# An expert tile's bias addition moved behind the next tile's first products, and three weight buffers instead of two

## The chip, the cores and the metric

The kernel runs on one core of a Trainium2 chip. The metric is the device time of one execution in microseconds, the median of three runs. A core has TensorE (PE in the profile; its weight loads are PEld), VectorE (DVE), ScalarE (ACT), GpSimd (POOL), SyncE (SP) and 16 DMA engines. Each engine executes its own queue of instructions in order, and engines wait for each other by semaphores.

## What is computed

The input x has four images of 256 channels and 64 by 64 pixels. Each image is normalised over its channels and goes through three modulated deformable 3x3 convolutions with a relu, and is added to x. Then every pixel is a token of 256 numbers: it is normalised, a gate picks its two best of eight experts, and each of the two contributes a two-layer network weighted by its gate value.

```python
def _deform_layer(x, w_off, b_off, w, b, dilation=1):
    om = lax.conv_general_dilated(x, w_off, ...) + b_off[None, :, None, None]
    off = om[:, :2 * K].reshape(B, K, 2, H, W)
    mask = jax.nn.sigmoid(om[:, 2 * K:])
    ...
    sampled = _bilinear(x, ys, xs) * mask[:, None]
    out = jnp.einsum('bikhw,oik->bohw', sampled, wk) + b[None, :, None, None]

x = x + _L0_conv_ref(_ln_c(x), ...)          # three of these layers, relu after each
t = _ln_t(_to_tokens(x))
probs = softmax(t @ gate_w + gate_b); top2_vals, top2_idx = top_k(probs, 2)
for each expert e:
    h = gelu(t @ W1[e] + b1[e]); y = h @ W2[e] + b2[e]
    out = out + cw[:, e] * y
x = _from_tokens(_to_tokens(x) + out)
```

All numbers are fp32.

## The kernel before

**Stages.** The convolution work is cut into 12 stages of one layer of one image, in the order of `stages` (line 1037): (0,0), (1,0), (0,1), (2,0), (1,1), (0,2), (2,1), (1,2), (0,3), (2,2), (1,3), (2,3), written as (layer, image). A stage has 8 blocks of 512 pixels; a block runs over 9 taps, a tap over 4 samples of 128 pixels. So a stage has 288 samples, and the run 3456.

**One sample** (`samples`, line 494): POOL issues an indirect DMA that gathers four corners for 128 pixels into a gather buffer g (L503; the pool `gat` has GB = 10 of them), VectorE sums the corners in two steps (L509, L514) into a buffer s (8 of them), ScalarE scales s in place (L517). Two samples are transposed on TensorE (`turn`, L532) and copied by ScalarE into sT (L535), and after four samples come the accumulating products with the layer's weights (`finish`, L555). `turn` is written LAG = 2 pairs behind the samples.

**Expert tiles.** When the third layer of an image is done its tokens are routed. The list of (token, expert) pairs, sorted by expert and padded, is cut into tiles of 256 rows: NF = 39 tiles for a whole image (groups 0, 1, 2) and 23 for each half of the last image (groups 3 and 4), 163 tiles in all. `begin` (line 968) puts each tile's generator `expert` into the lane `tiles` in three pieces, one every pace/3 taps; the pace is 5, 5, 2, 1.5 and 0 taps per tile for the five groups. Where no taps are left to run beside (`drain`, line 1021, called by `settle` and at the end) pieces are taken one after the other, and `draining` is set. The pieces of a tile are:

1. the bias addition of the tile before (`products`, L892, VectorE, from PSUM tile py to y) with the store of y on SP's queue (L895); then the transposes of the tile's 256 gathered tokens (L840) and ScalarE's copy fzT (L844);
2. when draining, the fetch for the next tile; then the first products ph (L856) and the Gelu hT (L866);
3. when not draining, the fetch for the next tile; then the second products py (L874).

`fetch` issues three indirect DMAs on POOL's queue: the weights of the tile's expert, both layers and biases, 9232 bytes a partition (L800), and two times 128 token rows zt (L812). The weight buffer w is one of two, by the parity of the step. A list `same` marks the tiles whose expert is that of the tile before them in the same stream; their row index lies beyond the bound, and nothing is moved. So that two streams can keep their weights, the list is worked on as two halves, alternating: `order` is tile 0, half, 1, half + 1 and so on, and `same` is set to 0 at the start of each half.

The py tile in PSUM is single (`ps1` has one buffer), so a tile's second products wait for the addition of the tile before. A weight buffer is free when its last reader, the addition with the bias of the second layer, is done.

**Order.** The code is traced by a framework that turns it into one queue per engine: it orders instructions by priority and readiness in its own plan, so an engine's order can differ from that of the code. `after(x)` keeps the instructions in its block behind x on their engine: the additions stand behind the newest sample's L514 (`self.last`), the fetches behind the newest gather (`self.gathered`).

The pool `wt` holds the weight tiles; before the first tile its buffers serve as windows of the convolution's input (`window`, line 281) in the first stage. In the first blocks the pool `gat` also lends buffers (`room`, line 188).

Of the kernel before, what the change touches and what calls it, by code (L numbers as in the profile page):

```python
# [34 lines left out]
FT_LOG = 8  # L35
FT = 1 << FT_LOG
FU = FT // P
GB = 10
LAG = 2
LEAST = 2.0**-30  # L40
WINN = CC * (RPB + 2) * W
W1N = CC * HID + HC
W2N = HC * C + C
# [39 lines left out]
class Group:  # L83


    def __init__(self, b, n0, n1):
        self.b, self.n0, self.n1 = b, n0, n1
        self.nm = f"{b}_{n0}"
        self.M = (n1 - n0) * TPB

        self.NF = 2 * self.M * P // FT + E - 1


        self.half = (self.NF + 1) // 2
        self.zt, self.acc, self.gy, self.sums, self.py = {}, [], [], [], None
        self.order = [s // 2 + s % 2 * self.half for s in range(self.NF)]


class Lane:
# [18 lines left out]
class Weave:  # L118
# [3 lines left out]
    def __init__(self, ctx, tc, ins, out):  # L122
        nc = self.nc = tc.nc
        self.tc = tc
        self.ins = ins
        self.x = ins["x"].rearrange("b (c p) h w -> b p c (h w)", p=P)
        self.out_v = out.rearrange("b (c p) h w -> b p c (h w)", p=P)
        self.B = self.x.shape[0]

        def pool(name, bufs, **kw):  # L130
            return ctx.enter_context(tc.tile_pool(name=name, bufs=bufs, **kw))

        self.cst = pool("cst", 1)
        self.dram = pool("dram", 1, space=bass.MemoryType.DRAM)
        self.wkp = pool("wkp", 1)
        self.plan = pool("plan", 19)
        self.win = pool("win", 3)
        self.wt = pool("wt", 2)
        self.small = pool("small", 1)
        self.big = pool("big", 2)  # L140
        self.ffn = pool("ffn", 2)
        self.rt = pool("rt", 1)
        self.rt2 = pool("rt2", 2)
        self.gyp = pool("gyp", 4)
        self.smT = pool("smT", 2)
        self.smp = pool("smp", 8)
        self.gat = pool("gat", GB)
        self.ps = pool("ps", 3, space=bass.MemoryType.PSUM)
        self.ps1 = pool("ps1", 1, space=bass.MemoryType.PSUM)

        self.routes, self.tiles, self.sums = Lane(), Lane(), Lane()
        self.side, self.plans_side = [], []
        self.last = self.gathered = self.turned = None
        self.starting, self.draining, self.later = True, False, []
        self.pend, self.pairs = None, []
# [534 lines left out]
    def route(self, grp):  # L690

        nc, M, NF = self.nc, grp.M, grp.NF
# [4 lines left out]
        def small(tag, shape, dt=F32):  # L697
            return self.rt.tile(list(shape), dt, tag=tag, name=f"{tag}_{grp.nm}")
# [52 lines left out]
        nc.vector.tensor_scalar(rows, ex, float(P), self.part, ALU.mult, ALU.add)  # L751
        same = small("same", (P, NF))
        nc.vector.tensor_tensor(same[:, 1:], ex[:, 1:], ex[:, : NF - 1], ALU.is_equal)
        nc.vector.memset(same[:, 0 : grp.half + 1 : grp.half], 0.0)
        nc.vector.scalar_tensor_tensor(rows, same, float(E * P), rows, ALU.mult, ALU.add)
        nc.vector.tensor_copy(grp.wrow, rows)

# [32 lines left out]
    def fetch(self, grp, step):  # L790

        if self.w is None:
            self.w = [
                self.wt.tile([P, 2, WINN], F32, tag="wt", name=f"w_{i}").rearrange(
                    "p a b -> p (a b)"
                )
                for i in range(2)
            ]
        f = grp.order[step]
        self.nc.gpsimd.indirect_dma_start(  # L800
            out=self.w[step % 2][:, : W1N + W2N],
            out_offset=None,
            in_=self.ins["W"],
            in_offset=bass.IndirectOffsetOnAxis(ap=grp.wrow[:, f : f + 1], axis=0),
            bounds_check=E * P - 1,
            oob_is_err=False,
        )
        grp.zt[step] = []
        for u in range(FU):
            zt = self.ffn.tile([P, C], F32, tag=f"zt{u}", name=f"zt_{grp.nm}_{f}_{u}")  # L810
            j = FU * f + u
            self.nc.gpsimd.indirect_dma_start(  # L812
                out=zt,
                out_offset=None,
                in_=grp.zd,
                in_offset=bass.IndirectOffsetOnAxis(ap=grp.tok[:, j : j + 1], axis=0),
            )
            grp.zt[step].append(zt)
# [6 lines left out]
    def expert(self, grp, step):  # L825

        nc = self.nc
        if step == 0:
            self.fetch(grp, 0)
            yield  # L830
        self.products(grp)
        f = grp.order[step]
        nm = f"{grp.nm}_{f}"
        w = self.w[step % 2]
        w1, w2 = w[:, :W1N], w[:, W1N : W1N + W2N]
        zt = grp.zt.pop(step)
        tp = self.ps.tile([P, CC, FT], F32, tag="tp", name=f"ftp_{nm}")
        for u in range(FU):
            for c in range(CC):
                nc.tensor.transpose(  # L840
                    tp[:, c, u * P : (u + 1) * P], zt[u][:, c * P : (c + 1) * P], self.ident
                )
        zT = self.ffn.tile([P, CC, FT], F32, tag="zT", bufs=1, name=f"fzT_{nm}")
        nc.scalar.copy(zT, tp)  # L844
        yield

        beside = not self.draining
        if not beside:
            self.fetch_next(grp, step)
        hT = []  # L850
        for h0 in range(0, HC, 2):
            ph = self.ps1.tile([P, 2, FT], F32, tag="ph", name=f"ph_{nm}_{h0}")
            for h in range(2):
                for c in range(CC):
                    o = c * HID + (h0 + h) * P
                    nc.tensor.matmul(  # L856
                        ph[:, h, :],
                        lhsT=w1[:, o : o + P],
                        rhs=zT[:, c, :],
                        start=(c == 0),  # L860
                        stop=(c == CC - 1),
                    )
            ht = self.ffn.tile([P, 2, FT], F32, tag="hT", bufs=3, name=f"hT_{nm}_{h0}")
            for h in range(2):
                k = CC * HID + h0 + h
                nc.scalar.activation(ht[:, h, :], ph[:, h, :], AF.Gelu, bias=w1[:, k : k + 1])  # L866
            hT.append(ht)
        yield
        if beside:
            self.fetch_next(grp, step)  # L870
        py = self.ps1.tile([P, FU, C], F32, tag="py", name=f"py_{nm}")
        for u in range(FU):
            for h in range(HC):
                nc.tensor.matmul(  # L874
                    py[:, u, :],
                    lhsT=hT[h // 2][:, h % 2, u * P : (u + 1) * P],
                    rhs=w2[:, h * C : (h + 1) * C],
                    start=(h == 0),
                    stop=(h == HC - 1),
                )  # L880
        grp.py = (f, py, w2)
# [254 lines left out]
```

## Time and profile before

| what | us |
|---|---|
| runs before | 7508.25 median of 3 (7496.17 to 7528.83) |
| profiled execution, whole | 7520.62 |
| its span, first to last instruction | 7518.9 |
| first addition y (L892) starts | 2377.0 |
| last gather (L503) issued | 7065.8 |
| last addition y starts | 7465.8 |

The mean granted clock of TensorE is 0.944. An engine's busy time is the time in which it executes something; "idle before" is its idle time just ahead of an instruction, put down to what ended it. "remote" and "another core or an unknown queue" mean that the profile does not name who ended a wait. Start times of the samples show the stages:

| stage | from | to | tiles' additions |
|---|---|---|---|
| (1,0), (0,1), (2,0) | 657 | 2110 | 0 |
| (1,1) | 2110 | 2652 | 7 |
| (0,2), (2,1), (1,2) | 2652 | 4472 | 39 |
| (0,3), (2,2) | 4472 | 5645 | 29 |
| (1,3) | 5645 | 6396 | 26 |
| (2,3) and the drain behind it | 6396 | 7519 | 62 |

### The profile page before, as it was taken

To read this page: it belongs to the slowest core of one execution; us is meant where nothing else is said; L and a number is where in the kernel's file an instruction comes from. 1 tells how busy PE (TensorE), PEld (TensorE's weight loads), DVE (VectorE), ACT (ScalarE), POOL (GpSimd) and SP (SyncE) were. 2 spreads that over 40 slices of the span, in tenths; PEclk is the share of its full clock that TensorE was granted. 3 is DMA by queue.
4 is the path that set the end of the run, shared out by engine and by line. 5 is a ranking of instruction groups with operands and counts; after the bars stand their busy time and mean duration, and the time that the engine had idled before them with its cause. 6 is when DMAs were issued, how large, how long until landed. Compare 5 with 4: busy or idle time off the path is not lost.

```text
span 7518.9 us, 88985 instructions
## 1 busy us (share of the span) xinstructions
PE 6443.2 (86%) x26500; PEld 3618.8 (48%) x26500; DVE 4952.9 (66%) x11467; ACT 3266.0 (43%) x7141; POOL 4476.5 (60%) x4245
## 2 busy tenths in 40 slices
PE   6898888888898888889988888888888788977887
PEld 3443333334454444445554445444544555644565
DVE  6776777768887666567777556666768554667421
ACT  3444544445544444445443434444444333444322
POOL 4654666656666565556557656555656565666543
PEclk8999999999999999999999999999999899989998
DMA  8997999989998888888888888888888777888644
GB/s 266 337 325 274 352 342 335 346 331 356 362 349 311 300 305 297 278 315 322 314 293 316 293 280 314 295 302 294 308 306 299 251 271 240 288 302 287 211 139 123
DMA packets 800320, 2223.73 MB, mean 296 GB/s; under 512 B 104729, under 2 KB 302873, under 8 KB 794081
## 3 DMA queue, kind: packets, MB, share of 16 engines
q0 software_dynamic: 551200, 1947.35, 73.3%
q1 hardware_dynamic: 248640, 270.69, 10.9%
q8 instruction: 215, 3.52, 0.2%
q14 instruction: 265, 2.16, 0.1%
HBM read 2160.68 MB, written 196.40 MB: 313 GB/s over the span
## 4 chain that ended last, share of the span: by engine, by line
PE 69%; ACT 10%; issue 7%; another core or an unknown queue 6%; DVE 4%; DMA 2%; POOL 1%; SPq 0%; ACTq 0%; DVEq 0%; POOLq 0%
PE acc L555 34%; PE tp L532 10%; PE ph L856 7%; PE py L874 6%; PE po L357 6%; ACT sT L535 4%; ACT s L517 3%; DVE g L509 2%; DVE s L514 1%; PE pm L371 1%; ACT hT L866 1%; PE ftp L840 1%; ACT win L577 1%; PE tpv L325 1%
## 5 line engine op out<-in xcount | busy, mean ns | idle before, releaser
L503 POOL DMA_INDIRECT g<-tab,idx x3456 | 3685.4, 1066 | 2371.6 <-DVE s L514 1061.8
L555 PE MATMUL acc<-sT,wk 128*128 128x512 f32 x6912 | 3492.1, 620 | 253.4 <-ACT sT L535 147.5
L509 DVE SCALAR_TENSOR_TENSOR g<-g,cf 128x512 f32<-128x512 f32 x3456 | 2559.2, 742 | 269.1 <-DMA g<-tab,idx 245.5
L514 DVE SCALAR_TENSOR_TENSOR s<-g,cf 128x256 f32<-128x256 f32 x3456 | 1662.7, 483 | 1331.3 <-PE tp L532 729.9
L535 ACT COPY sT<-tp 128x512 f32<-128x512 f32 x1728 | 1002.0, 585 | 2312.0 <-PE tp L532 1553.0
L517 ACT ACTIVATE s<-s,cf 128x256 f32<-128x256 f32 x3456 | 1629.5, 508 | 256.7 <-DVE s L514 160.7
L555 PEld LDWEIGHTS acc<-sT,wk 128*128 128x128 f32 x6912 | 1198.9, 198 | 1106.7 <-issue 816.7
L532 PEld LDWEIGHTS tp<-ident,s 128*128 128x128 f32 x6912 | 893.2, 146 | 1666.2 <-issue 898.9
L532 PE MATMUL tp<-ident,s 128*128 128x128 f32 x6912 | 1287.3, 286 | 439.2 <-ACT s L517 253.8
L856 PE MATMUL ph<-fzT,w 128*128 128x256 f32 x2608 | 720.8, 411 | 78.0 <-ACT fzT L844 28.1
L874 PE MATMUL py<-w,hT 128*128 128x256 f32 x2608 | 671.1, 396 | 103.5 <-ACT hT L866 58.0
L856 PEld LDWEIGHTS ph<-fzT,w 128*128 128x128 f32 x2608 | 506.3, 205 | 212.9 <-issue 69.6
L874 PEld LDWEIGHTS py<-w,hT 128*128 128x128 f32 x2608 | 484.5, 196 | 242.0 <-issue 91.9
L866 ACT ACTIVATE hT<-ph,w 128x256 f32<-128x256 f32 x652 | 281.9, 471 | 616.3 <-PE ph L856 378.2
L812 POOL DMA_INDIRECT zt<-z,tok x326 | 333.8, 1024 | 161.5 <-issue 88.0
L800 POOL DMA_INDIRECT w<-in_W,wrow x163 | 178.0, 1092 | 381.2 <-issue 138.8
L357 PE MATMUL po<-win,wo 128*32 128x504 f32 (+1 forms) x2304 | 366.0, 615 | 6.5 <-ACT win L301 4.2
L892 DVE TENSOR_TENSOR y<-py,w 128x512 f32<-128x512 f32 x163 | 111.9, 686 | 341.5 <-PE py L874 285.1
L915 POOL DMA_INDIRECT gy<-ys,slots x256 | 255.6, 998 | 104.5 <-issue 70.0
L930 DVE SCALAR_TENSOR_TENSOR ta<-gy,cw,ta 128x256 f32<-128x256 f32 x256 | 120.6, 480 | 125.6 <-DMA gy<-ys,slots 78.4
L357 PE MATMUL po<-win_pre,wo 128*32 128x504 f32 (+1 forms) x1152 | 184.2, 617 | 2.0 <-ACT om L366 2.0
L366 ACT ACTIVATE om<-po,bo 128x512 f32<-128x512 f32 x96 | 65.9, 687 | 265.3 <-PE po L357 156.3
(154 smaller groups left out, 2961.0 us busy)
## 6 DMA issues: line engine op xcount, KB each, us to landing
tab<-hv SPq DMA_DIRECT2D x512, 128.0 KB
g<-tab,idx POOLq DMA_INDIRECT x3456
ys<-y SPq DMA_DIRECT2D x163, 256.0 KB
tab<-h_pre SPq DMA_DIRECT2D x128, 256.0 KB
wk<-in_conv_w SPq DMA_DIRECT2D x99, 256.0 KB
xc_pre<-in_x SPq DMA_DIRECT2D x32, 512.0 KB
xr_tok<-in_x SPq DMA_DIRECT2D x32, 512.0 KB
t<-t_tok SPq DMA_DIRECT2D x32, 512.0 KB
```

Of the source, the lines that this page charges most:

```text
L357: nc.tensor.matmul(po[g * Q : (g + 1) * Q, :].rearrange("q (r w) -> q r w", w=W)[:, :, x0:x1], lhsT=self.wo[l][:, 3 * ky + kx, c, :], rhs= ...
L503: self.gathered = nc.gpsimd.indirect_dma_start(out=g.rearrange("p x s f -> p (x s f)"), out_offset=None, in_=self.table(*self.stages[i]), ...
L509: nc.vector.scalar_tensor_tensor(g[:, :, 0, :], g[:, :, 1, :], cf[:, j, 0:1], g[:, :, 0, :], ALU.mult, ALU.add,)
L514: self.last = nc.vector.scalar_tensor_tensor(s, g[:, 1, 0, :], cf[:, j, 1:2], g[:, 0, 0, :], ALU.mult, ALU.add)
L517: nc.scalar.activation(s, s, AF.Copy, scale=cf[:, j, 2:3])
L532: self.turned = nc.tensor.transpose(tp[:, c, u * P : (u + 1) * P], ss[u][:, c * P : (c + 1) * P], self.ident)
L535: nc.scalar.copy(self.sT[:, :, t0 * P : (t0 + 2) * P], tp)
L555: nc.tensor.matmul(acc[:, o, :], lhsT=self.wk[k][:, c, o * P : (o + 1) * P], rhs=sT[:, c, :], start=(k == 0 and c == 0), stop=(k == K - 1 ...
L812: self.nc.gpsimd.indirect_dma_start(out=zt, out_offset=None, in_=grp.zd, in_offset=bass.IndirectOffsetOnAxis(ap=grp.tok[:, j : j + 1], axi ...
L856: nc.tensor.matmul(ph[:, h, :], lhsT=w1[:, o : o + P], rhs=zT[:, c, :], start=(c == 0), stop=(c == CC - 1),)
L866: nc.scalar.activation(ht[:, h, :], ph[:, h, :], AF.Gelu, bias=w1[:, k : k + 1])
L874: nc.tensor.matmul(py[:, u, :], lhsT=hT[h // 2][:, h % 2, u * P : (u + 1) * P], rhs=w2[:, h * C : (h + 1) * C], start=(h == 0), stop=(h == ...
```

## The change

The list of tiles is worked on as three thirds, alternating, with three weight buffers; the gather pool has 9 buffers instead of 10. The addition of the tile before moves from the head of a tile's first piece to the head of its third, just ahead of the second products, with its store. The fetch for the next tile always stands at the head of the second piece, whether draining or not.

```diff
-GB = 10
+GB = 9
...
-        self.half = (self.NF + 1) // 2
+        self.third = -(-self.NF // 3)
...
-        self.order = [s // 2 + s % 2 * self.half for s in range(self.NF)]
+        self.order = [s // 3 + s % 3 * self.third for s in range(self.NF)]
...
-        self.wt = pool("wt", 2)
+        self.wt = pool("wt", 3)
...
-        nc.vector.memset(same[:, 0 : grp.half + 1 : grp.half], 0.0)
+        nc.vector.memset(same[:, 0 : 2 * grp.third + 1 : grp.third], 0.0)
...
-                for i in range(2)
+                for i in range(3)
...
-            out=self.w[step % 2][:, : W1N + W2N],
+            out=self.w[step % 3][:, : W1N + W2N],
...
         if step == 0:
             self.fetch(grp, 0)
             yield
-        self.products(grp)
         f = grp.order[step]
...
-        w = self.w[step % 2]
+        w = self.w[step % 3]
...
         nc.scalar.copy(zT, tp)
         yield
 
-        beside = not self.draining
-        if not beside:
-            self.fetch_next(grp, step)
+        self.fetch_next(grp, step)
         hT = []
...
             hT.append(ht)
         yield
-        if beside:
-            self.fetch_next(grp, step)
+        self.products(grp)
         py = self.ps1.tile([P, FU, C], F32, tag="py", name=f"py_{nm}")
```

## The prediction

> **What bounds the kernel now.** I read the page's busy shares first, then the same shares by stage, then the waits of VectorE and TensorE, then the lines of the change.
>
> ```profile
> PE 6443.2 (86%) x26500; PEld 3618.8 (48%) x26500; DVE 4952.9 (66%) x11467; ACT 3266.0 (43%) x7141; POOL 4476.5 (60%) x4245
> ```
>
> TensorE is the fullest engine. The stages tell whether it also sets the pace where the expert tiles run (columns: window, length, busy time of PE, PEld, DVE, ACT, POOL with counts, granted clock, DMA share, GB/s).
>
> ```profile
> 657.00:1129.00 472.00, 392.57 (x1457) 177.27 (x1452) 346.08 (x677) 219.46 (x484) 310.71 (x292) 0.96 0.93 343
> ...
> 2652.00:3240.00 588.00, 512.38 (x2087) 284.99 (x2086) 357.89 (x706) 257.59 (x574) 343.87 (x331) 0.96 0.86 295
> ...
> 5850.00:6400.00 550.00, 480.97 (x2058) 305.49 (x2057) 276.78 (x551) 215.04 (x485) 324.67 (x323) 0.94 0.77 260
> 6400.00:6660.00 260.00, 241.62 (x1031) 168.40 (x1030) 162.71 (x336) 116.13 (x255) 155.68 (x156) 0.97 0.85 293
> 6660.00:6920.00 260.00, 197.07 (x719) 105.59 (x718) 194.10 (x498) 106.65 (x222) 168.63 (x154) 0.90 0.87 300
> 6920.00:7067.00 147.00, 120.84 (x509) 84.70 (x507) 80.14 (x187) 57.75 (x123) 87.57 (x84) 0.94 0.74 251
> ```
>
> The first row is a stage without expert tiles (TensorE 83%), the second one with 15 (87%), the next two hold the dense tiles at a pace of 2 and 1.5 taps (87%, 93%), the fifth a routing phase without tiles, the last the end before the drain (82%). The last gather is issued at 7067; from there the tiles run alone.
>
> What a tile costs is read from the drain, in the timeline of VectorE:
>
> ```profile
> 7212.83 0.69 DVE L892 TENSOR_TENSOR y<-py,w 128x512 f32<-128x512 f32 x1 [7.56 <-PE py L874]
> 7221.03 0.69 DVE L892 TENSOR_TENSOR y<-py,w 128x512 f32<-128x512 f32 x1 [7.51 <-PE py L874]
> 7229.23 0.69 DVE L892 TENSOR_TENSOR y<-py,w 128x512 f32<-128x512 f32 x1 [7.51 <-PE py L874]
> ```
>
> A tile every 8.2 us. Fifteen tiles make 123 us, and 588 less 472 is 116: a stage with tiles is a stage without them plus TensorE's tiles. TensorE sets the pace; an idle VectorE is paid for only where TensorE runs dry too.
>
> **What the change aims at.** The bias addition waits for TensorE, with VectorE's gathered sums queued behind it. Total, times and longest wait, over the run:
>
> ```profile
> DVE y L892 <- PE py L874: 285.1, 49, 13.6
> DVE g L509 <- DMA g<-tab,idx: 245.5, 90, 10.9
> ```
>
> The same line cut at 7067 gives 100.8 us (20 times) before and 184.4 us after. After it, no sample is queued behind the addition: the 184.4 us cost nothing. Of the 100.8, all lie behind 5645, where the pace is 2 or 1.5 taps.
>
> **Part by part.**
>
> (a) *Addition later.* In the built order of group 2, 34 of 39 additions stand 9 samples behind the last sample transposed before their products; the new order has 8 at 9, 25 at 10 to 13. Eight buffers hold the scaled samples, so VectorE leads TensorE's transposes by at most 8: at 10 the products have always ended, at 9 they may not. Three quarters of the wait in this group goes. For groups 0 and 1 the distance goes from 13 to 21, where nothing waited. The bound is 0 to −100.8 us. TensorE is at 87 to 93% where most of these waits lie, no less than the 83 to 87% of stages without them; only the 147 us before the drain are low, at 82%. At 86% they would be 147 × 0.04 = 6 us shorter. I take −6. The wait removed from VectorE then becomes its wait for free sample buffers (L514 on the transposes, already 729.9 us), which is TensorE again.
>
> The Trainium skill ("Perfetto Trace Analysis", Identifying the Most-Contended Engine) says that matmul busy time is a bad measure of how full TensorE is, and names the weight loads' share instead. That share is 48% here, which would leave TensorE half free, make VectorE's 66% the fullest, and put the whole 100.8 us on the path: about 7407 us. The stage arithmetic above speaks against it here.
>
> (b) *Third weight buffer, fetch one piece earlier.* POOL's order decides: the weight fetch (L800) stands in POOL's queue with the gathers behind it, and waits until its buffer's last reader, an addition, is done. Before, at pace 2 and 1.5, the fetch stands 4 gathers behind that addition; in the new order, with three buffers, it still stands 4 behind it, since the addition has moved back by the piece count that the third buffer gives. At pace 5 it goes from 12 to 16, of 9 or 10 gather buffers: no stall either way. So POOL's lead over VectorE stays short in the dense stages (median 7.9 us from the end of a gather's issue to its use in stage (1,3), against 12.5 to 16 us in the others), and the 227.7 us of waits for gathers behind 5645 stay. Effect 0. Per tile POOL issues the same three fetches (L800 once, L812 twice; 163 and 326 in all), each about 1.05 us, one piece earlier; behind them in the queue only the order changes. In the drain, where no gather separates them, the weights can be fetched a tile of 8.2 us earlier. What they cost there:
>
> ```profile
> PE otp L948 <- issue: 20.5, 10, 3.3
> PE otp L948 <- DVE ta L930: 16.6, 6, 8.4
> PE py L874 <- ACT hT L866: 14.9, 21, 7.9
> PE ph L856 <- DMA w<-in_W,wrow: 14.2, 4, 7.6
> ```
>
> That is TensorE's waits behind 7067: 14.2 us in four waits, the bound of the gain. I take −12. Against it stands a forced third weight load at the start of each group (five more loads in the run). In the dense stages it lies beside TensorE; in the drain's one or two groups I take +4, half a wait of 7.6 us (bounds 0 and 2 × 7.6 = 15). Together −8, between −14 and +15.
>
> (c) *Second products later.* In groups 0 and 1 the old order begins a tile's second products as soon as the Gelu allows, and TensorE waits 43 us for the Gelu before 7067 (23.6 behind 5645, 19.5 before). The new order begins them 8 to 12 samples later (the second tile's behind sample 1315 instead of 1307), right behind the addition, long after the Gelu. Bound 0 to −43. What they filled elsewhere is lost, so I take a quarter: −10.
>
> (d) *New wait of TensorE for VectorE.* The products now stand right behind an addition that VectorE executes 1 or 2 samples later than the last transposed one. Behind the products in TensorE's queue lie the transposes and the accumulation (L532, L555). Where VectorE leads by several samples, the addition is over. Where TensorE has caught up, VectorE needs 0.74 + 0.48 + 0.69 = 1.91 us (L509, L514, L892) while ACT's 0.51 and four transposes of 0.15 take 1.1 us: 0.8 us a tile. The 729.9 us that VectorE waits for transposes show it ahead nearly everywhere. Bounds 0 and 125 tiles before the drain × 0.8 = +100; taken +2, the row nearest (TensorE's wait for y in the drain, 2.3 us).
>
> (e) *Nine gather buffers.* Where the lead is 12.5 to 16 us, one of ten buffers is one sample period, 472/288 = 1.64 to 606/288 = 2.1 us. Transfers there waited for (short leads) landed in 3 to 4 us. The cover is that lead; 0 taken. Without it each of the 90 waits for a gather could grow by 2.1 us: +189 us of VectorE, nothing below 0.
>
> (f) *Windows.* The third buffer is also free for the pre-windows of stage (0,0), where VectorE waited 10.0 us once at L292; between 0 and −10, taken −1, TensorE being the bound.
>
> SP's store of y (0.4 us an issue, 163) moves with the addition. SP waits there 1152.2 us in 80 waits for y, with table stores and weight taps behind; a shorter wait of y shortens this one. Taken 0.
>
> Sum: −6 − 8 − 10 + 2 + 0 − 1 = −23 us. The profiled execution took 7520.6 us (span 7518.9): 7498. The runs' median is 7508.25, 12 us lower; from it 7485 us, which I predict.
>
> **Rivals.** *Nothing reaches TensorE* (7508): (a) to (c) are all idle time of engines off the path. For it: 93% at 6400 in spite of the waits. Against: the drain's 14.2 us are on TensorE itself.
>
> *The starved stages pay* (7428): TensorE runs dry wherever VectorE waits there, and gets it all back; 7508 − 100.8, and + 20.7 for the 8 of 39 places still at 9 samples. For it: gathers wait longest exactly where y waits. Against: TensorE's share there.
>
> *TensorE waits for the addition* (7583): (d) at three quarters of its upper bound, +75. Its place is the first of the second products of each tile; it decides where VectorE leads by fewer than 2 samples. For it: TensorE waits for scaled samples already (140.7 us between 2304 and 5645), so it does catch up. Against: those waits are 88, on some 800 transposed pairs.
>
> **Chances and range.** Forecast 0.45, nothing reaches TensorE 0.18, starved stages pay 0.17, TensorE waits for the addition 0.20. A measurement of this kernel tells about 0.5%, 38 us, from no change (its runs spread from 7496 to 7529). With ±25 us around each case, faster by more (below 7471): 0.17 of the second rival but for a hundredth, plus 0.3 of the forecast, 0.30; slower (above 7546): 0.20; within: 0.50. The likeliest case's own range is 7455 to 7515. The range 7418 to 7576 leaves out some 0.18, parts of both outer rivals.
>
> **What would show it.** Right: y's wait before 7067 falls from 100.8 to about 30 us; fetch L800 still ends long waits in stages (1,3) and (2,3); waits for w in the drain shrink from 14.2 us; stages without tiles keep 472, 481 and 500 us. Wrong: a new row "PE py waits for DVE y" of tens of us; waits for gathers in stages before 5645; or TensorE's share above 90% in the last third and a time below 7455.

## The result, and the profile after

The changed kernel takes 7557.56 us (median of 9 runs, 7536.64 to 7588.9), the kernel before, run beside it, 7500.98 us (9 runs, 7487.89 to 7528.83). The ratio is 1.0073, with a 95% interval of 1.0052 to 1.0095: slower by 0.7%, 55 us. The forecast was 7485 us, a gain of 0.3%.

The page's first line after the change, by engine, reads almost as before:

```profile
PE 6452.2 (85%) x26500; PEld 3620.0 (48%) x26500; DVE 4954.1 (66%) x11467; ACT 3270.2 (43%) x7141; POOL 4484.4 (59%) x4245
```

The loss is found by cutting the span into four: up to stage (1,3), stage (1,3), stage (2,3) up to the last gather, and the drain. Before (columns as in the prediction's table of stages):

```profile
97.00:5645.00 5548.00, 4815.27 (x19533) 2543.25 (x19534) 3916.08 (x8930) 2554.22 (x5588) 3399.39 (x3181) 0.95 0.89 316
5645.00:6396.00 751.00, 642.32 (x2699) 400.30 (x2701) 435.37 (x969) 297.37 (x654) 445.85 (x427) 0.93 0.78 265
6396.00:7066.00 670.00, 563.54 (x2280) 360.78 (x2268) 438.44 (x1022) 282.27 (x604) 413.98 (x397) 0.94 0.83 286
7066.00:7519.00 453.00, 358.63 (x1574) 282.92 (x1574) 105.25 (x285) 104.49 (x232) 190.61 (x195) 0.88 0.44 135
```

After:

```profile
97.00:5652.00 5555.00, 4812.56 (x19520) 2537.71 (x19520) 3916.98 (x8931) 2556.48 (x5590) 3403.85 (x3181) 0.95 0.89 315
5652.00:6431.00 779.00, 649.58 (x2694) 404.91 (x2694) 434.51 (x967) 296.30 (x653) 444.33 (x428) 0.91 0.75 257
6431.00:7116.00 685.00, 574.96 (x2318) 369.04 (x2318) 443.47 (x1035) 288.03 (x611) 421.82 (x399) 0.93 0.82 283
7116.00:7552.00 436.00, 349.17 (x1546) 275.52 (x1544) 101.57 (x271) 101.72 (x225) 187.39 (x192) 0.89 0.45 139
```

The four lengths change by +7, +28, +15 and −17 us: the drain pays, and the two stages in which tiles come every 2 or 1.5 taps take it back more than twice.

What becomes of VectorE's waits in stage (1,3) says why nothing was won there. Before (engine, what waited and for whom, total us, times, longest):

```profile
DVE g L509 <- DMA g<-tab,idx: 143.1, 38, 10.9
DVE y L892 <- PE py L874: 44.9, 9, 7.7
...
DVE s L514 <- PE tp L532: 18.2, 8, 9.2
...
DVE s L514 <- remote: 15.2, 6, 6.8
```

After:

```profile
DVE s L514 <- remote: 99.5, 30, 9.7
DVE s L514 <- PE tp L532: 74.3, 33, 9.7
DVE g L509 <- DMA g<-tab,idx: 51.6, 29, 5.2
DVE y L888 <- PE py L870: 29.9, 4, 10.9
```

The waits for gathers fall by 91.5 us and those for the addition by 15. The waits ahead of L514, which needs a free sample buffer, grow by 140.4 us, of which the profile names TensorE for 56.1 and no one ("remote") for 84.3: VectorE now has more of its samples and stands, as far as it is named, behind TensorE. The stage itself takes 28 us longer, and TensorE's longest waits there name ScalarE:

```profile
PE tp L532 <- ACT sT L535: 23.2, 8, 8.7
PE tp L532 <- ACT s L517: 20.9, 13, 8.4
PE ph L853 <- ACT fzT L843: 19.8, 5, 7.5
```

Before, they were 3.5, 7.1 and 4.5 us. Over the stages with tiles (2304 to the last gather) TensorE's waits for scaled samples go from 174.2 to 216.0 us, and those of the window products for the copies sT from 56.8 to 69.1.

One of e3's six executions below took 9271.97 us at a granted clock of 0.657, and no ratio uses it.

### The profile page after: what moved, and what is told of

The parts are those of the page before. It is cut to its first block, busy times and chain, and to the rows that moved or that the text cites. A ratio compares the mean times of both kernels' runs of the same rounds, so it can differ in the third digit from the quotient of the medians.

```text
span 7552.5 us, 89157 instructions
## 1 busy us (share of the span) xinstructions
PE 6452.2 (85%) x26500; PEld 3620.0 (48%) x26500; DVE 4954.1 (66%) x11467; ACT 3270.2 (43%) x7141; POOL 4484.4 (59%) x4245
## 4 chain that ended last, share of the span: by engine, by line
PE 67%; ACT 9%; issue 8%; another core or an unknown queue 7%; DVE 5%; DMA 2%; POOL 1%; SPq 0%; ACTq 0%; DVEq 0%; POOLq 0%
PE acc L555 33%; PE tp L532 10%; PE ph L853 7%; PE py L870 6%; PE po L357 6%; ACT sT L535 4%; ACT s L517 3%; DVE g L509 2%; DVE s L514 1%; PE pm L371 1%; DMA g<-tab,idx 1%; ACT hT L863 1%; ACT win L577 1%; PE tpv L325 1%
## 5 line engine op out<-in xcount | busy, mean ns | idle before, releaser
L514 DVE SCALAR_TENSOR_TENSOR s<-g,cf 128x256 f32<-128x256 f32 x3456 | 1662.7, 483 | 1516.2 <-PE tp L532 791.5
L853 PE MATMUL ph<-fzT,w 128*128 128x256 f32 x2608 | 683.5, 402 | 84.1 <-ACT hT L863 28.0
L870 PE MATMUL py<-w,hT 128*128 128x256 f32 x2608 | 631.7, 391 | 37.9 <-ACT hT L863 23.6
```

The source lines that it names most:

```text
L514: self.last = nc.vector.scalar_tensor_tensor(s, g[:, 1, 0, :], cf[:, j, 1:2], g[:, 0, 0, :], ALU.mult, ALU.add)
L853: nc.tensor.matmul(ph[:, h, :], lhsT=w1[:, o : o + P], rhs=zT[:, c, :], start=(c == 0), stop=(c == CC - 1),)
L870: nc.tensor.matmul(py[:, u, :], lhsT=hT[h // 2][:, h % 2, u * P : (u + 1) * P], rhs=w2[:, h * C : (h + 1) * C], start=(h == 0), stop=(h == ...
```

## The experiments

The runs come in five sets. Each set ran on one chip, with the kernel before beside it, and each on a chip of its own. Times of different chips are not compared here, only ratios to the kernel before on the same chip. The times are medians; the ratios are estimated from all runs of a set and lie up to 0.0014 from the quotients of the medians.

| run | kernel | us | before, us | ratio | 95% interval |
|---|---|---|---|---|---|
| e1 | 9 gather buffers alone | 6810.84 | 6807.77 | 1.0009 | 1.0001 to 1.0018 |
| e2 | third weight buffer alone | 6741.08 | 6807.77 | 0.9904 | 0.9888 to 0.9919 |
| e3 | third buffer, fetch early | 6767.65 | 6807.77 | 0.9944 | 0.9930 to 0.9959 |
| e4 | third buffer, addition late | 6779.70 | 6807.77 | 0.9964 | 0.9951 to 0.9977 |
| e5 | the changed kernel | 7559.43 | 7504.93 | 1.0068 | 1.0055 to 1.0082 |
| e6 | as e2 | 7482.22 | 7504.93 | 0.9974 | 0.9961 to 0.9987 |
| e7 | changed, addition at the end of piece 2 | 7543.75 | 7504.93 | 1.0040 | 1.0025 to 1.0055 |
| e8 | changed, second products in halves | 7528.52 | 7504.93 | 1.0032 | 1.0018 to 1.0046 |
| e9 | as e3 | 7676.29 | 7632.82 | 1.0057 | 1.0035 to 1.0079 |
| e10 | as e4 | 7609.09 | 7632.82 | 0.9966 | 0.9945 to 0.9986 |
| e11 | e2, second products in one stretch | 7645.88 | 7632.82 | 1.0014 | 0.9994 to 1.0035 |
| e12 | e8, fetch where it stood | 7614.04 | 7632.82 | 0.9979 | 0.9955 to 1.0003 |
| e13 | the changed kernel | 7646.00 | 7628.17 | 1.0009 | 0.9985 to 1.0032 |
| e14 | as e2 | 7583.46 | 7628.17 | 0.9937 | 0.9915 to 0.9960 |
| e15 | as e3 | 7667.15 | 7628.17 | 1.0053 | 1.0032 to 1.0075 |
| e16 | as e4 | 7597.00 | 7628.17 | 0.9964 | 0.9942 to 0.9986 |
| e17 | changed, window products ordered | 6674.27 | 6810.04 | 0.9804 | 0.9791 to 0.9818 |
| e18 | e2, window products ordered | 6685.53 | 6810.04 | 0.9825 | 0.9811 to 0.9838 |

### First set: the change taken apart (e1 to e4)

e1 is the kernel before with one line changed:

```diff
-GB = 10
+GB = 9
```

> The kernel before with nine gather buffers instead of ten, nothing else. Theory A (the place of the bias addition: behind it TensorE's queue is interleaved worse, so that a tile's second products cut a pair of transposes in two and first products stand right behind the copy they need): no change, ratio 0.998 to 1.002 to the kernel before (7501 us), since the order of the engines is that of before. Theory B (the ninth buffer is missed, POOL's lead over VectorE is too short): about the whole loss of the change, ratio 1.006 to 1.008, 7550 us or more, with longer waits of VectorE for gathers. The prediction put this at 0.

e2 has the change's lines for nine gather buffers, three weight buffers and three thirds, with addition and fetch where the kernel before has them. Against the changed kernel:

```diff
         if step == 0:
             self.fetch(grp, 0)
             yield
+        self.products(grp)
...
-        self.fetch_next(grp, step)
+        beside = not self.draining
+        if not beside:
+            self.fetch_next(grp, step)
         hT = []
...
         yield
-        self.products(grp)
+        if beside:
+            self.fetch_next(grp, step)
```

> Three weight buffers, thirds and nine gather buffers, but the addition at the head of the first piece and the fetch in the third piece, as before. In the built order the fetch now stands 12 gathers behind the addition that frees its buffer at a pace of 2 taps (4 before). Theory A: not slower than before, and faster by what POOL's stalls were worth: ratio 0.993 to 1.000, stage (1,3) shorter than 751 us, its waits for gathers (138 us in the trace before) mostly gone. Theory B: ratio 1.006 or more, like the change. Theory C (the third weight load of the thirds, five more loads, costs it in the drain): about 1.002 to 1.004, the loss behind 7067 us.

e3 takes only the first of these edits (addition where it stood, fetch early), e4 only the fetch's (addition late, fetch where it stood, at the head of the third piece).

> The changed kernel with the addition put back to the head of the first piece; fetch in the second piece, three buffers, nine gather buffers. The fetch stands 8 gathers behind the addition it waits for at a pace of 2 taps. Theory A: the loss goes, ratio to before 0.994 to 1.001. Theory D (the earlier place of the fetch: three more DMA issues ahead of gathers at a bad moment): ratio 1.004 to 1.008, as the changed kernel. Theory B: 1.006 or more.

> The changed kernel with the fetch put back to the third piece when tiles run beside the samples (second piece in the drain, as before); the addition stays just ahead of the second products. Theory A: the loss stays, ratio to before 1.004 to 1.010, stages with tiles longer by 5 to 30 us each. Theory D: the loss goes, ratio 0.998 to 1.002. If POOL's stall were the loss (fetch 4 gathers behind the addition in the changed kernel, 8 here): ratio near 1.000.

The tenth gather buffer is worth about 0.1%. The third weight buffer alone gains 1.0%: it is the part of the change that pays. In VectorE's waits from the start of (1,3) to the end, e1 first:

```profile
DVE g L509 <- DMA g<-tab,idx: 286.1, 140, 9.9
```

and e2:

```profile
DVE g L509 <- DMA g<-tab,idx: 90.3, 61, 6.3
```

The fetch now stands 12 gathers behind the addition that it waits for at the pace of 2 (in the built order; 4 before), and (1,3) falls from 688 to 652 us, (2,3) with the drain from 1021 to 994. The Trainium skill ("Perfetto Trace Analysis", Optimization Strategy) says that a gap that keeps coming back on the engine that should be saturated can mean too little room for the next tile, by the number of buffers among other things. The two rows show such gaps shrink with one buffer more, from 286.1 to 90.3 us, though on VectorE and not on the engine that sets the pace.

Either move then takes part of this gain away: the early fetch 0.0040, the late addition 0.0060. Their sum would put the changed kernel at 1.0004 on this chip; the changed kernel itself has no run there.

### Second set: the changed kernel beside its base (e5 to e8)

> The changed kernel itself, beside the others on one chip. If the two losses seen apart simply add up (addition late: 0.9964 - 0.9904 = +0.0060 of the time before; fetch early: 0.9944 - 0.9904 = +0.0040), it stands at 0.9904 + 0.0100 = 1.0004 of the time before here. If the two hurt each other more than their sum (a fetch only 4 gathers behind the late addition at the quick pace, a wait in GpSimd's queue), it stands at 1.004 to 1.010, as where it was first measured (1.0073). If it is under 0.998 here, the loss belongs to the chip with the lower granted clock and not to the order.

> Three weight buffers and three thirds with the addition and the fetch where they stood before: 0.9904 of the time before in the first comparison. Its gain was in the two starved stages, waits of VectorE for gathers behind a stalled weight fetch, so it should be there on any chip: 0.986 to 0.994. If it is within 0.5% of 1 here, that gain belongs to the clock of one chip.

e7 moves one line of the changed kernel to the other side of the last piece's start:

```diff
             hT.append(ht)
-        yield
         self.products(grp)
+        yield
```

> The changed kernel with the addition one piece earlier, ahead of the end of the first products' piece and behind its matmuls; all else as changed. The order it gives on TensorE: pairs of sample transposes that are cut by second products fall from 51 to 9, but sample pairs whose copy has no matmul between it and the window product that needs it rise from 208 to 234 of 864. Theory A1 (second products that cut a sample pair cost the time): 0.5% less than the changed kernel. Theory A2 (copies without cover cost it): no less than the changed kernel, rather 0.2% more. Theory D (the weight fetch stands too near behind the addition it waits for, here 8 gathers at the quick pace, there 4): 0.3 to 0.6% less, and the gain in the two starved stages (1,3) and (2,3) alone.

e8 issues a tile's second products for u = 0 in the third piece, and those for u = 1 at the head of the next tile's first piece (or ahead of the last addition):

```diff
+        self.second_rest()
         f = grp.order[step]
...
-        for u in range(FU):
-            for h in range(HC):
...
         grp.py = (f, py, w2)
+        self.second(py, hT, w2, 0)
+        self.rest = (py, hT, w2, 1)
```

> The changed kernel with each tile's second products in two halves of eight matmuls, the second half in the next tile's first piece; additions and fetches stand where the change has them. Second products lie in 2 to 4 stretches again, as before, not in one. If their lying in one stretch of 16 matmuls is what costs (samples wait while it runs, and the copies around it have no cover), the dense stages fall by 5 to 10 us each and the time to 0.5% below the changed kernel. If it is the place of the addition or of the fetch, the time stays within 0.2% of the changed kernel.

The changed kernel is 0.0094 over the third buffer alone here, about the 0.0100 of the first chip's sum. So there are two parts of opposite sign: a buffer that gains and moves that lose more. The size of the first depends on the chip: 0.26% here, 0.96% there.

e7 comes 0.28% back and e8 0.36%. e7 is instructive in stage (1,3): the waits for gathers are gone (2 us), and the stage still takes 783 us against 791 in e5 and 756 in e6. VectorE's waits for gathers are therefore not all that makes (1,3) long. Still, (1,3) and (2,3) fall by 8 and 13 us against e5, where theory D looked for its gain, and theory A2 (copies without cover, 234 instead of 208) expected no gain at all. e8's larger part back speaks for the one stretch in which the changed kernel's second products lie, but its stages fell unevenly: (0,2), (0,3) and (1,3) by 13 to 16 us, while (2,1) and (2,3) rose by 19 and 23.

### Third set: each move again, and the stretch by itself (e9 to e12)

> Three buffers, addition where it stood, fetch one piece earlier: the fetch's move alone. On the first chip it took 0.0040 of the time from the third buffer's gain (0.9904 to 0.9944). Where the third buffer stands at 0.9974 and the changed kernel at 1.0068: 1.000 to 1.003 if the fetch's move costs the same there; 0.997 to 0.999 if it costs nothing by itself; 1.005 or more if it makes most of the change's loss.

> Three buffers, addition just ahead of the next second products, fetch where it stood: the addition's move alone (with the order of second products that it brings). On the first chip it took 0.0060. Where the third buffer stands at 0.9974 and the changed kernel at 1.0068: 1.002 to 1.005 if the two losses add up; 1.006 or more if it makes all of the loss; under 0.999 if it costs nothing there.

e11 leaves addition and fetch of e2 alone and turns round the order of the sum in the second products, so that the first of them needs the last Gelu:

```diff
-            for h in range(HC):
+            for h in reversed(range(HC)):
...
-                    start=(h == 0),
-                    stop=(h == HC - 1),
+                    start=(h == HC - 1),
+                    stop=(h == 0),
```

> The third buffer with addition and fetch where they stood, and the second products' sum taken from the last hidden slice to the first: the same 16 matmuls, but the first of them needs the tile's last Gelu, so that they come to lie in one stretch in 113 of 163 tiles (third buffer 60, changed kernel 123), and 214 sample copies have no matmul between them and their window product (195 and 208). If the one stretch is what costs in the changed kernel, this is 0.3 to 0.5% slower than the third buffer alone: 1.000 to 1.003 of the time before where that stands at 0.9974 (0.993 to 0.996 where it stands at 0.9904). If the place of the addition itself or of the fetch costs it, this stays within 0.15% of the third buffer alone.

e12 is e8 with the fetch as in e4.

> The addition late, but second products in two halves (the second in the next tile's first piece) and the fetch where it stood. If one stretch and the early fetch are the two costs, both are gone and it stands within 0.2% of the third buffer alone: 0.996 to 0.999 where that stands at 0.9974. If the addition's place has a cost of its own, as it makes the next second products wait, it stays 0.4% or more above it. By the static order its uncovered sample copies are 234, more than any but the late addition's own; if these are what costs, it is no faster than the late addition with one stretch.

The weights turn round: on this chip the early fetch loses to the kernel before (1.0057), and the late addition stays ahead of it (0.9966). Both came again on another chip in the fourth set. e11 stands at 1.0014. The third buffer alone was not run on this chip: against e6's 0.9974 that is 0.4% lost, as expected, and against 0.9937 on a chip of almost the same time (e14) 0.8%, with no buffer, addition or fetch moved. Only the order in which TensorE's and the other queues were built differs. e12 went as the last sentence of its expectation has it: no faster than the late addition with one stretch, so the stretch is not a cost that can simply be taken away by halves.

### Fourth set: all four corners side by side (e13 to e16)

> The changed kernel, in one comparison with the third buffer alone, the fetch's move alone and the addition's move alone, all against the kernel before on the same chip. It stood at 1.0073 and 1.0068 on two chips. If the chip is one of the lower granted clocks (time before near 7500 us or above): 1.005 to 1.009. If it is the quick one (near 6810 us): 0.998 to 1.002.

> The third buffer alone, the common base of the other three. 0.9904 of the time before on the quick chip, 0.9974 on a slower one, by waits of VectorE for gathers that are gone in the two starved stages. Expected: 0.994 to 0.999 on a chip of lower clock, 0.989 to 0.992 on the quick one.

> The fetch's move alone on that base. Theory F (the fetch's early place makes most of the change's loss on a chip of lower clock, in stage (1,3) above all, where every kernel with the early fetch took 778 to 793 us and those with the late one 751 to 761): 0.6 to 1.0% over the third buffer beside it, and within 0.3% of the changed kernel. Theory S (two moves, each some 0.5%, that add up): 0.4 to 0.6% over the third buffer, and 0.4% under the changed kernel. On the quick chip both give 0.4% over the third buffer, as seen.

> The addition's move alone on that base. Theory F: within 0.2% of the third buffer beside it. Theory S: 0.4 to 0.6% over it. On the quick chip 0.6% over it, as seen.

| against the third buffer alone | fetch where it stood | fetch early |
|---|---|---|
| addition where it stood | 0.9937 (base) | 1.0053: +0.0116 |
| addition late | 0.9964: +0.0027 | 1.0009: +0.0072 |

The early fetch costs most, as theory F has it, and theory S falls: the moves don't add up here, for the late addition takes 0.0044 of the early fetch's loss back. Theory F doesn't hold in full either: it wanted the early fetch within 0.3% of the changed kernel and the late addition within 0.2% of the base (its interval overlaps the base's). The changed kernel alone came out within the noise of the kernel before here (expected 1.005 to 1.009); its loss against its base is there on both chips that had the two.

Where the losses lie shows in the profiled executions, stage by stage (start times of the samples; us more than in the base, with e17 and e18 of the fifth set):

| kernel less base | up to (1,1) | (0,2) to (2,2) | (1,3) | (2,3) | drain |
|---|---|---|---|---|---|
| early fetch, e15 less e14 | +21 | +40 | +16 | −9 | +10 |
| late addition, e16 less e14 | +9 | −13 | +5 | +4 | +10 |
| both, e13 less e14 | +7 | −4 | +24 | +36 | −1 |
| both, e5 less e6 | +17 | +8 | +35 | +25 | −3 |
| both, window products ordered, e17 less e18 | +5 | −23 | +3 | +25 | −9 |

Parts of 10 us mean little: (0,0), where no tile runs, differs by as much between e15 and e14. The early fetch alone loses most in the five stages from (0,2) to (2,2), not in (1,3) as theory F has it; and e11, whose fetch is late, took 781 us in (1,3), outside the 751 to 761 us that theory F gives for a late fetch. The changed kernel loses some 60 us in (1,3) and (2,3) on both chips. In these two VectorE's waits for gathers are 127 us in e5 and 119 in e13, against 15 and 16 in their bases: the fetch that stands 4 gathers behind its addition gives back about half of what the third buffer takes off these waits (227.7 us in the kernel before). e7, with 18 us of them, has 40 us of the 60 left, so this is at most a part of the loss.

The early fetch shows no wait of its own: in (1,3) VectorE waits 2 us for gathers in e15, 5 us in e14. In the five stages ahead of it the wait that differs most stands on TensorE, in window products that wait for ScalarE's copy. In the five stages from (0,2) to (2,2), base e14 first, then e15, e16 and e13:

```profile
PE acc L555 <- ACT sT L535: 27.5, 29, 3.0
```

```profile
PE acc L555 <- ACT sT L535: 74.4, 59, 11.8
```

```profile
PE acc L555 <- ACT sT L535: 46.5, 59, 3.0
```

```profile
PE acc L555 <- ACT sT L535: 46.6, 46, 10.4
```

The rows are least in the base and most with the early fetch, as the four times are, but the five stages that they were read in took 3025, 3065, 3012 and 3021 us: only the early fetch's 47 us go with a longer time. On the first chip the rows are 21.3 us in e2, 36.7 in e3 and 51.7 in e4, for five stages of 2631, 2651 and 2667 us. Yet TensorE's idle time there, all waits together, is 151, 152 and 175 us, so that e3's 20 us stand in TensorE's busy time, 2480 and 2499 us. In the built order 195 of 864 window products of the base have no matmul between the last transposition of their samples and themselves, so that TensorE stands still while ScalarE copies; 213 with the early fetch, 234 with the late addition, 208 with both. The count doesn't give the size of the loss, for the late addition has the most and loses the least. That these waits are what the moves cost is not shown.

### Fifth set: the waits taken away in both (e17, e18)

e17 is the changed kernel, e18 is e2, both with one line more in `finish`:

```diff
+        with self.after(self.turned):
             for o in range(CC):
                 for c in range(CC):
                     nc.tensor.matmul(
                         acc[:, o, :],
```

The window products then stand behind the newest sample transposition, which is one tap further on. In the built order no window product is left directly behind its own copy, and 278 (e17) and 408 (e18) sample pairs are cut by other work, where it was 992 and 1067. GpSimd's order is the same, instruction for instruction, as in the changed kernel and in e2. (The expectations speak of six dense stages and of a third chip: the waits that they name were read in the five stages above, 25 us in e6 and 27.5 in e14, and the 86 us in the five stages ahead of them, in e6 and e14 alike.)

> The changed kernel with each window product ordered behind the newest sample transposition: the static order then leaves no window product directly behind the copy that it reads (208 of 864 before), and 278 sample pairs are cut by other work instead of 992. Theory U (what addition and fetch cost is that they push TensorE's order into waits for ScalarE's copies): the wait of window products for the copies falls from 46 to 62 us in the six dense stages with tiles to under 10 us, and the kernel comes to 0.3% or less of the third buffer with the same order (e18). Theory Q (the cost is in GpSimd's queue, the weight fetch behind the late addition): the wait falls as well, but this stays 0.6% or more over e18, most of it in stages (1,3) and (2,3). Whether the order is itself quicker than the one before is open: fewer cut pairs may also leave VectorE's sample buffers occupied longer; 0.98 to 1.02 of the time before.

> The third buffer alone with the same ordering of window products (195 uncovered copies before, none now; cut pairs 1067 before, 408 now). Theory U: within 0.3% of e17. Theory Q: 0.6% or more under e17. By itself: if the waits for copies cost what they show (25 us in the six dense stages, 86 us in the five before them on the third chip), some 1% less than the third buffer alone without it; if the order only moves the wait to TensorE's next transposes, no change.

The rows of the page for the window products and the sample transposes, and its first line, for e2 (line, engine, operation, count, busy us, mean ns, idle before):

```profile
PE 6193.3 (92%) x26500; PEld 3520.7 (52%) x26500; DVE 4960.8 (74%) x11467; ACT 3264.7 (48%) x7141; POOL 4439.4 (66%) x4245
...
L555 PE MATMUL acc<-sT,wk 128*128 128x512 f32 x6912 | 3387.6, 604 | 150.4 <-ACT sT L535 136.6
...
L532 PE MATMUL tp<-ident,s 128*128 128x128 f32 x6912 | 1247.8, 281 | 178.7 <-ACT s L517 164.2
```

for e18:

```profile
PE 6105.5 (91%) x26500; PEld 3590.2 (54%) x26500; DVE 4953.1 (74%) x11467; ACT 3273.7 (49%) x7141; POOL 4390.2 (66%) x4245
...
L556 PE MATMUL acc<-sT,wk 128*128 128x512 f32 x6912 | 3172.5, 600 | 3.3 <-ACT win L578 2.6
...
L532 PE MATMUL tp<-ident,s 128*128 128x128 f32 x6912 | 1100.6, 281 | 302.4 <-ACT s L517 291.2
```

and for e17:

```profile
PE 6113.9 (92%) x26500; PEld 3605.3 (54%) x26500; DVE 4973.2 (74%) x11467; ACT 3272.7 (49%) x7141; POOL 4400.1 (66%) x4245
...
L556 PE MATMUL acc<-sT,wk 128*128 128x512 f32 x6912 | 3166.3, 598 | 7.4 <-ACT win L578 5.4
...
L532 PE MATMUL tp<-ident,s 128*128 128x128 f32 x6912 | 1072.9, 281 | 298.6 <-ACT s L517 288.6
```

The waits of the window products for copies are gone, but TensorE doesn't wait less: its waits ahead of the sample transposes rise by 124 us from e2 to e18, and its idle time in all (span less busy time) is 545 of 6738.3 us in e2 and 578 of 6683.7 in e18. What falls is its busy time, by 88 us. So the waits moved to the transposes, and the gain of 0.8% lies in TensorE's busy time. Its products now follow each other with fewer cuts; that this is the reason is argued, not shown.

The moves' loss is gone in the sum: the changed kernel is now 0.0021 under its base, within 0.3% as theory U has it, where the first quick chip's two parts summed to 0.0100 over it. Theory Q needed at least 0.006 over. With GpSimd's order unchanged in both, the price of the moves depends on the order of the other queues, and TensorE's is the one that was changed here. But theory U's mechanism, the waits for copies, is not shown by this, since these waits only moved. And by stage theory Q's part is there: e17 takes 25 us more than e18 in (2,3), with 229 us of VectorE's waits for gathers in (1,3) and (2,3) against 95, and makes it good in the five stages before.

Both versions beat the kernel before on their chip: 6674.27 us against 6810.04 is 2% less, the best version of this study. What stays open: the pair ran on a quick chip only, where the early fetch costs 0.4% and not 1.2%; the changed kernel without the line has no run on a quick chip; and the kernel before with this line alone was not tried.

## Why the prediction was wrong

**What failed.** The time lies inside the stated range, 7418 to 7576, but on the wrong side of no change, and only because the range takes in most of the rival "TensorE waits for the addition"; that rival's mechanism did not occur, so it is luck. The steps that failed are the prices of the moves in (b) and (c). Step (b) took the fetch's move as 0 outside the drain, because "behind them in the queue only the order changes". Step (c) noted "What they filled elsewhere is lost" and still took −10. Neither priced what the new places do to the order of the queues around the samples, TensorE's above all. The one term for a new wait of TensorE, the +2 of (d), was sought at the second products, where they wait for VectorE's addition; that wait is 2.3 us in the whole run, 2.2 of it in the drain, so (d) was right in itself.

In their place the runs showed this. Put against the base on one chip, addition and fetch together cost +0.0072 and +0.0094 of the time, 55 and 71 us, where (a), (c) and (d) stood at −14 us and the fetch at 0. (The −12 us of the drain belong to the third buffer: while draining, the fetch stands in the second piece in both kernels.) Some 60 us of the loss lie in (1,3) and (2,3). The same moves cost nothing in sum when TensorE's window products are ordered otherwise (e17, e18). Which waits carry the loss stays open: returning waits for gathers are a part at most (e7), and the waits for ScalarE's copies go with the time of their stages in some kernels and not in others.

**(a) Addition later: wrong.** The wait of y before the last gather was to fall from 100.8 to about 30 us. It went to 95.5, in 11 waits instead of 20, the longest 14.2 instead of 9.2. The step read the built order of group 2, most of which runs in stage (1,3), and there y's wait did fall, from 44.9 to 29.9 us. But the larger part of the 100.8 us lay in (2,3), and it rose from 55.9 to 65.6. The first half group's eight additions there, which the step left out, stood 5 to 7 samples behind their products' last transposition; in the new order every second one stands at 10 or more and waits for nothing, and the others stand at 5 or 6 and wait 11 to 14 us each. The rule of the step, that at 10 samples nothing waits any more, agrees with this; its count left out the group with the longer waits.

**(b) Third buffer and fetch: two errors of opposite sign.** The drain was right in sign and place: TensorE's wait there for weights fell from 14.2 to 2.1 us, and the drain is 17 us shorter (forecast 8). In its rows after the change:

```profile
PE py L870 <- ACT hT L863: 23.6, 24, 5.6
...
PE py L870 <- DVE y L888: 2.2, 2, 1.4
PE ph L853 <- DMA w<-in_W,wrow: 2.1, 1, 2.1
```

In the dense stages the buffer was taken as 0, since in the changed kernel the fetch still stands 4 gathers behind its addition. That is true of the changed kernel, but it hid what the buffer is worth without the moves: 0.26, 0.63 and 0.96% on three chips (e6, e14, e2). So the moves had more to lose than the prediction saw. And the early fetch was 0 in the sum, and is +0.0040 on one chip and +0.0116 on another. The waits for gathers behind 5645, which the step left at 227.7 us, fell by about half, to 51.6 and 71.6 us in the two stages, without a gain in time.

**(c) Second products later: the wait went, the gain did not.** TensorE's wait for the Gelu ahead of second products, 43.1 us before the last gather, is gone: the 23.6 us that are left in the whole run (row above) all lie in the drain. But in the same stretch first products now wait 26.7 us for the Gelu (12.0 before), and the samples and window products wait longer, as shown. The step also put the whole 43 us down to groups 0 and 1; only the 19.5 us before 5645 lie where these groups run.

**(e) Nine gather buffers** was right: e1 is at 1.0009. (The 90 transfers that were waited for landed a median 4.5 us behind the end of their issue, 3.0 to 7.3, and not 3 to 4.) **(f)**: VectorE's waits for windows in the first stage went from 20.0 to 13.5 us, the one at L292 gone, and the stage took 559 and 550 us.

**The stage arithmetic held.** TensorE sets the pace: where VectorE's waits for gathers fell by 91.5 us in (1,3), longer waits ahead of L514 took their place, on TensorE where they are named, and the stage became longer. The rule of the Trainium skill that was weighed ("Perfetto Trace Analysis", Identifying the Most-Contended Engine) speaks of how close TensorE is to its roofline, and names MFU (the share of peak arithmetic) beside the weight loads' share. Read as the prediction read it, it would have put VectorE first and the time at 7407 us. The measured 7557.56 doesn't decide this, as y's wait hardly fell; stage (1,3) speaks against that reading, where VectorE's waits for gathers and for the addition fell by 106.5 us and the time rose by 28, with the weight loads' share at 48% before and after. The stages without tiles kept their 472, 480 and 500 us (475, 475, 496).

**The rivals.** "TensorE waits for the addition" (7583 us) came nearest in time, but its mechanism is not what happened: no wait of py for y appeared. "The starved stages pay" was hardly tested, as y's wait before the last gather fell by 5 us alone. What was missing was a rival that priced the built order of TensorE's whole queue: the order was at hand for the queues of additions, fetches and second products, and the prediction counted distances only there.

## What to carry to other kernels

Where a planner orders the queues, moving one small step reorders its neighbours on the engine that sets the pace; read in the built order what becomes of that engine's other work, not only the distances of the moved step. Take a change with several parts apart before judging any: here a buffer that gains and moves that lose more hid behind one ratio near 1. When one wait is gone, add up the engine's idle and busy time before saying what was won: one line that put independent transposes between a copy and its reader took 0.8% off the base (0.9904 to 0.9825, on two chips of one time), and TensorE's idle time rose by 33 us while its busy time fell by 88.

## What the runs showed of the hardware

The same kernel before took 6808 and 6810 us on two chips, 7505 on a third, 7628 and 7633 on two more: 12% between the ends. The granted clock of TensorE differed less, 0.982 in e2 against 0.946 in e6 and 0.940 in e14, the same kernel. On the slower chips TensorE also stands still for what the profile doesn't name. In e14, from (0,2) to (2,2):

```profile
PE tp L532 <- issue: 104.2, 51, 8.4
```

In e2 no such row is among the seven listed, of which the least is 3.6 us. An order's worth differed with the chip: the early fetch cost 0.4% on a quick chip and 1.2% on a slow one, the late addition 0.6% and 0.3%. A comparison of kernels has to be made on one chip.
